# A macaron block with two routed expert layers: fewer steps of routing per group, deeper buffers for its scatters, and weight loads that wait for gathers

## The chip, the cores and the metric

The kernel runs on one core of one Trainium2 chip. The core has five engines that run their own instruction lists side by side and wait for each other through semaphores: TensorE (PE, matrix products and transposes), VectorE (DVE), ScalarE (ACT), GpSimd (POOL) and SyncE (SP), which here only issues transfers. Transfers (DMAs) run on 16 DMA engines that all queues share. The metric is the device time of the whole kernel in microseconds (us); lower is better. Everything is computed in float32, except for some small products of the softmax in bfloat16.

## The reference: what is computed

The input x has 8 sequences of 1024 rows of 512 numbers, so 8192 rows (tokens). Three residual steps follow each other:

```python
x = x + 0.5 * _L0_ffn_ref(_layernorm(x, axis=-1), w_router, w_gate, w_up, w_down)
x = x + _L0_attn_ref(_layernorm(x, axis=-1), Wq, bq, Wk, bk, Wv, bv, Wo, bo)
x = x + 0.5 * _L0_ffn_ref(_layernorm(x, axis=-1), w_router, w_gate, w_up, w_down)
```

The feed-forward step is a mixture of 32 experts, and each token goes to one of them, the one with the largest router logit. An expert takes at most C = 320 tokens, in the order of the tokens; a token beyond that gets only its own normalized row back. The expert's result is weighted by the token's softmax probability:

```python
logits = xt @ w_router
top1 = jnp.argmax(probs, axis=-1)
pos = jnp.cumsum(onehot, axis=0)[jnp.arange(T), top1] - 1
slot = jnp.where(pos < C, top1 * C + pos, E * C)
y = silu(buf @ w_gate) * (buf @ w_up) @ w_down        # per expert
```

The attention step is 16 heads of width 32 with rotary positions over each sequence.

## The kernel before, in words

The kernel has four stages in time: the front (0 to about 155 us of the profile) routes all tokens for the first expert layer; the first expert stage runs to about 960 us; attention to about 4065 us, and inside it the routing for the second layer; then the second expert stage until the end.

**The front** (`front`, L339) handles the 8192 tokens as 64 tiles of 128 rows. Its loop runs over the tiles with different parts of the work at different distances: SyncE loads four tiles at a time (`load(t)`, L353, 1 MB each, tile `xq`); VectorE takes mean and variance 12 tiles ahead (`stats`, L149: L151 and L152, tiles `st` and `mv`); for each group of 4 or 8 tiles `normalizing` (L154) makes the scale: VectorE adds the epsilon (`rstd`, L162), GpSimd raises to the power -0.5 (L163), VectorE makes `nmr` and two more (L165 to L167); ScalarE normalizes a tile to `h` (L172); TensorE transposes it (`tp`, L194); ScalarE, or for each eighth tile VectorE, copies the transposed tile to `xT` (L408); `routers` (L214) makes the logits of four tiles with two products (`pl` L223, `lp` L235) and copies (`parts` L230, `lg` L240).

Then `route` (L243) works on one group of 4 or 8 tiles. VectorE finds the maximum `mx`, the exponent's argument `ex`, the chosen expert as a one-hot row `oh`, and the running count `run` (L271 to L285). TensorE counts the tokens ahead of each one (`pp`, L290 and L294). VectorE makes from it the position `pos`, the table entry `row` (token number and gate, L304 and L305) and the place in the table, `slot` (L314 to L322), and for tokens beyond C the place `spare` (L324, L327). GpSimd scatters the entries into a table in HBM, one indirect transfer of 128 entries for each tile (L331). A group can start only when the group before has its `run`. There are ten groups, of 4, six times 8, and three times 4 tiles.

The routing is written as Python generators. Each `yield` ends a step, and `advance` (L391), which is called once in each turn of the loop over tiles, lets every open generator take one step. So a `yield` puts the rest of the routing into the next turn, behind the next tile's work, in each engine's list; engines work their lists strictly in order. The yields have three kinds (`WAIT`, `PE`, `DVE`), which the front does not tell apart. After the last tile `advance` is called until nothing is left.

After the last `run`, `sorted` (L433) sorts the experts by load (`keys` to `matrix`, then `order` and `arm`, L444 to L471). The order of the experts decides which weights are loaded first. An expert has three matrices, `wg`, `wu` and `wd`, of 1 MB each; `load` (L475) reads the expert's number into SyncE and issues three loads. After `front`, the weights of the first two experts of the first stage are loaded into a pool of their own (`et`, L1409 and L1430), so these loads stand in SyncE's list ahead of the stage. A load starts when SyncE reaches it and its buffer is free.

**An expert stage** (`experts`, L489) first reads the table back (`slots`, L553, issued by SyncE; it waits for the scatters), brings it into the experts' order with two small products (L557), and has the row numbers `come` and `go` (L559 to L564). Then for each expert GpSimd gathers its up to 320 rows with three indirect transfers (`gather`, L603, L609, tile `x`). `begin` (L568) normalizes and transposes the first expert's rows; it has three more powers on GpSimd. Then the loop over the experts: `feed` (L700) makes `gp` and `up` (L692) from the transposed rows `bT` and `wg`, `wu`, then `yp` (L731, L739) with `wd`, and prepares the next expert's rows meanwhile. In the loop the weights of expert r+1 are loaded and the rows of expert r+2 gathered. The pool `ew` (L509) has two sets of weights. In the first stage SyncE also loads each expert's share of all rows (`all`, L622) for the tokens beyond C, and GpSimd scatters them (L637); results are scattered at L749.

The orders of TensorE, ScalarE, VectorE and GpSimd are as written; SyncE's order is made by the framework's scheduler, which places an issue where its data and buffers are expected to be ready.

Of the kernel before, what the change touches and what calls it, by code (L numbers as in the profile page):

```python
# [13 lines left out]
F32 = mybir.dt.float32  # L14
I32 = mybir.dt.int32
# [7 lines left out]
P = 128  # L23
# [5 lines left out]
G = 8  # L29
# [3 lines left out]
WAIT, PE, DVE = "wait", "pe", "dve"  # L33
# [17 lines left out]
class Block:  # L51
# [191 lines left out]
    def route(  # L243
        self, t0, lg, pool, psum, tag, carry, table, spare=None, apart=False, counted=None
    ):

        nc, E, C, G = self.nc, self.E, self.C, lg.shape[1]
        rev = self.rev[:, 0:G, :]

        def wide(name):
            return pool.tile([P, G, E], F32, tag=name, bufs=2 if apart else 1, name=name)

        def narrow(name, dtype=F32):
            return pool.tile([P, G], dtype, tag=name, bufs=2, name=name)  # L260

        def over_e(x):
            return x.unsqueeze(2).to_broadcast([P, G, E])

        token = self.token[:, t0 : t0 + G]
        ex, oh = wide("ex"), wide("oh")
        mx, se, m = narrow("mx"), narrow("se"), narrow("m")

        row = pool.tile([P, G, 2], F32, tag="row", name="row")
        yield DVE, 1.5  # L270
        nc.vector.tensor_reduce(mx, lg, AX.X, ALU.max)  # L271

        nc.vector.tensor_tensor(ex, lg, over_e(mx), ALU.subtract)
        nc.scalar.activation(ex, ex, AF.Exp)
        nc.vector.tensor_tensor(lg, lg, over_e(mx), ALU.is_equal)
        nc.vector.tensor_tensor(lg, lg, rev, ALU.mult)
        yield DVE, 1.6
        nc.vector.tensor_reduce(m, lg, AX.X, ALU.max)
        nc.vector.tensor_tensor(oh, rev, over_e(m), ALU.is_equal)


        run = pool.tile([P, G + 1, E], F32, tag="run", bufs=2, name="run")
        nc.vector.tensor_copy(run[:, 0, :], carry)
        for j in range(G):
# [19 lines left out]
        nc.vector.tensor_scalar(row[:, :, 1], se, 0.5, None, ALU.mult)  # L304
        nc.vector.tensor_copy(row[:, :, 0], token)  # L305
        pos, s, u = narrow("pos"), narrow("s"), narrow("u")
        slot = narrow("slot", I32)
        nc.vector.tensor_reduce(pos, lg, AX.X, ALU.add)
        yield DVE, 1.5
        if order:  # L310
            at_once(order)

        tokens = slice(t0, t0 + G)
        nc.vector.tensor_scalar(u, pos, float(P), None, ALU.is_ge)  # L314
        for i in range(2, self.NB):
            nc.vector.scalar_tensor_tensor(u, pos, float(i * P), u, ALU.is_ge, ALU.add)
        nc.vector.scalar_tensor_tensor(s, m, float(-P), pos, ALU.mult, ALU.add)
        nc.vector.scalar_tensor_tensor(s, u, float((E - 1) * P), s, ALU.mult, ALU.add)

        nc.vector.tensor_tensor(s, s, self.away[:, tokens], ALU.subtract)  # L320
        nc.vector.scalar_tensor_tensor(s, pos, float(C), s, ALU.is_lt, ALU.mult)
        nc.vector.tensor_tensor(slot, s, self.past[:, tokens], ALU.add)  # L322
        if spare is not None:
            nc.vector.scalar_tensor_tensor(  # L324
                u, pos, float(C), self.beyond[:, tokens], ALU.is_ge, ALU.mult
            )
            nc.vector.tensor_scalar(spare[:, tokens], u, float(self.T), None, ALU.add)  # L327
        for j in range(G):
            if apart and j % 2 == 0:
                yield WAIT, 1  # L330
            nc.gpsimd.indirect_dma_start(  # L331
                out=table[t0 + j],
                out_offset=bass.IndirectOffsetOnAxis(ap=slot[:, j : j + 1], axis=0),
                in_=row[:, j, :],
                in_offset=None,
            )
        return run[:, G, :]

    def front(self, pool, psum, x, rest, spare, carry, table, ranked):  # L339
# [4 lines left out]
        nc, NT, D, KD, E = self.nc, self.NT, self.D, self.KD, self.E  # L344
# [4 lines left out]
        r, n = (pool.tile([P, NT], F32, name=name, bufs=1) for name in ("rstd", "nmr"))  # L349
# [2 lines left out]

        def load(t):  # L353
            xs[t // 4] = xq = pool.tile([P, 4, D], F32, tag="xq", bufs=7, name="xq")
            nc.sync.dma_start(
                xq, x[t * P : (t + 4) * P, :].rearrange("(j p) d -> p j d", p=P)
            )

        def tile_of(t):
            return xs[t // 4][:, t % 4, :]  # L360
# [7 lines left out]
        def routed(g):  # L368

            def counted(counts):  # L370
                state.carry = counts
                state.next += 1
                if state.next == len(sizes):
                    return ranked(counts)

            while state.next < g:
                yield
            yield from self.route(
                starts[g], lgs[g], pool, psum, "lp", state.carry, table, spare, True, counted
            )  # L380
# [10 lines left out]
        def advance():  # L391
            for steps in list(work):
                try:
                    next(steps)
                except StopIteration:
                    work.remove(steps)

# [4 lines left out]
        for i in range(-ahead, NT + 2):  # L402
# [3 lines left out]
            if late:  # L406
                to, from_, t = late
# [14 lines left out]
            t = i + ahead  # L422
# [49 lines left out]

        return (matrix, order, arm), rest()

    def load(self, pool, order, r, weights):  # L475

        nc = self.nc
        e = nc.values_load(
            order[0:1, r : r + 1], engines=[mybir.EngineType.SP], min_val=0,
            max_val=self.E - 1, skip_runtime_bounds_check_because="the number of a column of E",  # L480
        )
        tiles = []
        for name, w in zip(("wg", "wu", "wd"), weights):
            t = pool.tile([P, w.shape[1] // P, w.shape[2]], F32, tag=name, name=name)
            nc.sync.dma_start(t, w.rearrange("e (k p) f -> e p k f", p=P)[e])
            tiles.append(t)
        return tiles

    def experts(self, table, ranks, src, dst, weights, loaded=(), others=None):  # L489

# [7 lines left out]
        nc, tc, E = self.nc, self.tc, self.E  # L498
# [7 lines left out]
        for i in tc.Switch(which, len(self.profiles)):  # L506
            widths = self.profiles[i]
            with (
                tc.tile_pool(name="ew", bufs=2) as wp,  # L509
                tc.tile_pool(name="ea", bufs=2) as ap,  # L510
                tc.tile_pool(name="eps", bufs=2, space=PSUM) as ps,
                tc.manual_schedule(engines={F.PE, F.Activation, F.DVE, F.Pool}),
            ):
                expert = Expert(self, (wp, ap, ps), src, views, others)
                expert.places(table, matrix)

                def load(r):
                    return loaded[r] if r < len(loaded) else self.load(wp, order, r, weights)

                now = expert.gather(0, widths[0])  # L520
                now.weights = load(0)
                expert.begin(now)
                following = expert.gather(1, widths[1])
                for r in range(E):
                    if following:
                        following.weights = load(r + 1)
                    after = None
                    if r + 2 < E:
                        after = lambda: expert.gather(r + 2, widths[r + 2])
                    now, following = following, expert.feed(now, following, after)  # L530
# [842 lines left out]
def tile_macaron(  # L1373
# [3 lines left out]
    nc = tc.nc  # L1377
# [28 lines left out]

    F_ = mybir.EngineType
    first = ExitStack()
    et = first.enter_context(tc.tile_pool(name="et", bufs=2))  # L1409
    with (  # L1410
        tc.tile_pool(name="a", bufs=2) as pool,
        tc.tile_pool(name="aps", bufs=4, space=PSUM) as psum,
# [14 lines left out]
            return steps  # L1427

        s.front(pool, psum, xf, rest, spare, zero, dram_disjoint_views(tables[0], NT), ranked)
        loaded = [s.load(et, ranks[1], r, weights) for r in range(2)]  # L1430

    s.experts(tables[0], ranks, xf, x1, weights, loaded, (*rest, spare))
    first.close()
# [50 lines left out]
```

## Time and profile before

| what | us |
|---|---|
| time, median of 3 runs | 4916.72 (4915.27 to 4916.75) |
| profiled execution, its own time | 4919.01 |
| profiled execution, span | 4917.2 |
| TensorE busy in the span | 4646.1 (94%) |
| first statistics of a row (L151) | at 7.19 |
| first and last scatter of the first table (L331) | at 46.02 and 154.57 |
| first table read back (L553), issued | at 162.65 |
| first gather (L609), first product gp (L692) of the first stage | at 174.14 and 187.18 |
| last scatter of the second table | at 4074.51 |
| second table read back, issued | at 4077.49 |
| first gather, first product gp of the second stage | at 4082.05 and 4094.90 |
| granted clock of TensorE, mean | 0.971 |

The times in the lower rows count from the start of the span. A span is what the profiler saw between the first and the last instruction; the execution's own time is 1.8 us more. In the profile a line of the chain of work says what the last work was waiting for at that time; a "wait" names the instruction that came last of those waited for. The mark "issue" stands for time that no wait explains. The landing time of a transfer runs from its issue to the event that says that its data is there.

### The profile page before, as it was taken

What the parts mean: (1) busy time and instruction counts of PE and PEld (TensorE: products, weight loads), DVE (VectorE), ACT (ScalarE), POOL (GpSimd) and SP (SyncE); (2) the same over time, 40 slices, a digit from 0 to 9 for tenths busy, and PEclk for the clock granted to TensorE, in tenths of its full rate; (3) what the DMA queues carried; (4) which work ended last, traced back from release to release, by engine and by line L of the source; (5) the groups of instructions that cost most, each with busy time, mean ns of one, the idle gap of its engine ahead of it and who ended that gap; (6) DMA issues with size and microseconds to landing.
All of it is one profiled execution on the core that took longest, in us unless ns stands there. A gap on an engine that the chain in (4) does not pass through costs nothing.

```text
span 4917.2 us, 68877 instructions
## 1 busy us (share of the span) xinstructions
PE 4646.1 (94%) x24572; PEld 2133.2 (43%) x24572; DVE 2847.5 (58%) x5568; ACT 2925.1 (59%) x5856; POOL 789.9 (16%) x784
## 2 busy tenths in 40 slices
PE   7599999969899999999999999999999877999998
PEld 4366667723233333333333333333333224666676
DVE  8333333346666767777767767767777633333332
ACT  7121112118998888888888888888888831111111
POOL 4332333210000010110110010100001002222221
PEclk8799999979999999999999999999999988999999
DMA  4455556530111212212212212212212124445554
GB/s 140 154 171 169 195 181 212 193 91 22 37 31 55 76 38 67 70 42 64 69 42 66 70 40 67 70 38 67 63 46 57 48 67 164 161 155 170 169 183 135
DMA packets 290534, 486.03 MB, mean 99 GB/s; under 512 B 47847, under 2 KB 83121, under 8 KB 290176
## 3 DMA queue, kind: packets, MB, share of 16 engines
q1 hardware_dynamic: 255328, 404.36, 26.1%
q0 software_dynamic: 34560, 76.93, 5.1%
q8 instruction: 196, 3.21, 0.3%
q14 instruction: 162, 1.33, 0.1%
q10 hardware_dynamic: 288, 0.20, 0.0%
HBM read 380.11 MB, written 89.72 MB: 96 GB/s over the span
## 4 chain that ended last, share of the span: by engine, by line
PE 81%; DVE 8%; ACT 4%; issue 3%; DMA 2%; POOL 1%; SPq 1%; DVEq 0%; POOLq 0%; ACTq 0%
PE sa L1206 13%; PE gp L692 10%; PE up L692 9%; PE pq L1111 9%; PE po L1288 9%; PE yp L731 9%; PE sb L1186 5%; PE pv L1156 4%; PE px L1314 4%; PE sb L1213 3%; ACT junk L1225 2%; DVE nm L1221 2%; PE tp L680 2%; PE tp L194 1%; PE yp L739 1%
## 5 line engine op out<-in xcount | busy, mean ns | idle before, releaser
L1221 DVE TENSOR_REDUCE nm<-sa 128x2 f32<-128x1024 f32 x1024 | 1248.9, 1221 | 648.8 <-PE sa L1206 388.8
L1225 ACT ACTIVATE junk<-sa,nm 128x512 f32<-128x512 f32 x2048 | 1408.2, 688 | 256.2 <-DVE nm L1221 177.5
L1206 PE MATMUL sa<-k,q 32*128 32x512 f32 x4096 | 1150.0, 645 | 19.4 <-ACT junk L1225 12.0
L1218 ACT ACTIVATE pr<-sb 128x1024 f32<-128x1024 f32 x1024 | 1041.4, 1019 | 102.7 <-PE sb L1213 98.8
L1213 PE MATMUL sb<-q,k 32*128 32x512 f32 x4096 | 1063.2, 603 | 0.0
L697 ACT ACTIVATE sg<-gp 128x320 f32<-128x320 f32 (+3 forms) x256 | 102.9, 402 | 1231.2 <-PE gp L692 1081.3
L1136 POOL TENSOR_TENSOR raw<-raw,a 128x512 f32<-128x512 f32 x128 | 164.8, 1288 | 2398.7 <-DMA rot<-raw 1770.9
L1288 PE MATMUL po<-pr,v 128*32 128x512 f32 x4096 | 549.7, 608 | 0.1
L692 PE MATMUL gp<-bT,wg 128*128 128x320 f32 (+3 forms) x2048 | 533.4, 404 | 0.5 <-DVE bT L600 0.5
L692 PE MATMUL up<-bT,wu 128*128 128x320 f32 (+3 forms) x2048 | 525.8, 400 | 0.0
L1111 PE MATMUL pq<-hT,wqk 128*128 128x512 f32 x1024 | 511.4, 624 | 4.6 <-DVE raw L1126 3.6
L731 PE MATMUL yp<-wd,a 128*128 128x512 f32 x1024 | 453.7, 596 | 0.0
L692 PEld LDWEIGHTS gp<-bT,wg 128*128 128x128 f32 x2048 | 387.8, 191 | 116.7 <-issue 28.4
L1186 PE MATMUL sb<-mrow,ones 3*128 3x512 bf16 x2048 | 393.0, 385 | 40.4 <-ACT pr L1218 39.0
L692 PEld LDWEIGHTS up<-bT,wu 128*128 128x128 f32 x2048 | 389.8, 190 | 95.0 <-issue 1.4
L716 DVE TENSOR_TENSOR a<-sg,up 128x320 f32<-128x320 f32 (+3 forms) x256 | 114.1, 446 | 541.7 <-PE up L692 509.2
L1186 PEld LDWEIGHTS <-ones 3*128 3x128 bf16 x2048 | 99.6, 91 | 708.7 <-issue 668.4
L1225 ACT ACTIVATION_READ_ACCUMULATOR junk<-sa,nm 128x1 f32 x2048 | 398.1, 194 | 0.0
L1213 PEld LDWEIGHTS sb<-q,k 32*128 32x128 f32 x4096 | 359.9, 184 | 0.1
L1206 PEld LDWEIGHTS sa<-k,q 32*128 32x128 f32 x4096 | 305.1, 184 | 82.7 <-ACT pr L1218 31.3
L1111 PEld LDWEIGHTS pq<-hT,wqk 128*128 128x128 f32 x1024 | 176.2, 191 | 323.5 <-issue 227.4
L735 DVE SCALAR_TENSOR_TENSOR ys<-yp,gates,x 128x512 f32<-128x512 f32 x128 | 96.1, 751 | 369.0 <-PE yp L731 369.0
(176 smaller groups left out, 4277.4 us busy)
## 6 DMA issues: line engine op xcount, KB each, us to landing
wg<-in_w_gate SPq DMA_DIRECT2D x64, 1024.0 KB
wu<-in_w_up SPq DMA_DIRECT2D x64, 1024.0 KB
wd<-in_w_down SPq DMA_DIRECT2D x64, 1024.0 KB
rot<-raw SPq DMA_DIRECT2D x1024, 32.0 KB
xq<-in_x SPq DMA_DIRECT2D x16, 1024.0 KB
all<-in_x SPq DMA_DIRECT2D x32, 512.0 KB
xt<-first_rows SPq DMA_DIRECT2D x64, 256.0 KB
xr<-first_rows SPq DMA_DIRECT2D x64, 256.0 KB
```

The source lines that it names most:

```text
L692: nc.tensor.matmul(acc, w[:, k, f * P : (f + 1) * P], to.bT[:, k, 0:width], start=(k == 0), stop=(k == s.KD - 1),)
L731: nc.tensor.matmul(yp, a[:, f, i * P : (i + 1) * P], wd[:, f, :], start=(f == 0), stop=(f == KF - 1),)
L1111: nc.tensor.matmul(acc, w[:, which, k, :], self.hT[b, n][:, k, :], start=(k == 0), stop=(k == KD - 1),)
L1156: nc.tensor.matmul(acc, hT[:, k, at : at + P], self.w_vo[:, k, :], start=(k == 0), stop=(k == KD - 1),)
L1186: nc.tensor.matmul(sb[:, h, :], self.ones16[at : at + 3, :], row[at : at + 3, :], start=True, stop=False,)
L1206: nc.tensor.matmul(sa[:, h, :], qa[at, (g * 4 + j) * P : (g * 4 + j + 1) * P], ka[at, m * 512 : (m + 1) * 512], start=True, stop=True,)
L1213: nc.tensor.matmul(sb[:, h, :], k[at, t * P : (t + 1) * P], q[at, n * 512 : (n + 1) * 512], start=False, stop=True,)
L1218: nc.scalar.activation(pr, sb, AF.Exp)
L1221: nc.vector.tensor_reduce(nm[:, m, j, pair : pair + 2], sa, AX.X, ALU.max, negate=True)
L1225: nc.scalar.activation(self.junk, sa[:, h - pair, :], AF.Exp, bias=nm[:, m, j, h : h + 1], accum_out=se[:, m, j, h : h + 1],)
L1288: nc.tensor.matmul(self.po[at : at + HD, :], self.v[b][t][:, c * P + at : c * P + at + HD], prs[h // 2 * 2][:, h % 2, :], start=(t == 0), ...
L1314: nc.tensor.matmul(acc, self.oT[b, c, half][:, j * P : (j + 1) * P], self.w_vo[:, c, :], start=False, stop=(c == KD - 1),)
```

## The change

There are four edits in the front and two at the expert stages.

1. In the front, `advance` lets a generator run on over yields of the kinds `PE` and `DVE` and stops it only at a `WAIT`. One `WAIT` is added in `route`, between the two VectorE parts at the start. So routing of a group takes fewer turns of the loop. The waiting loop in `routed` yields a `WAIT` too.
2. In the front's routing, `row` and `slot` get four buffers each instead of two. In attention, where `route` is used as well, they keep two.
3. The first load of four tiles is split into four loads of one tile.
4. Only the first expert's weights are loaded after the front, not those of two; the pool `et` has one set.
5. In the first stage, the second expert's weights are loaded by the loop into `ew`. Its `wg` gets a GpSimd memset of one element first, which stands in GpSimd's list behind the second expert's gathers. The load writes the same tile, so it waits for the memset, and what stands behind it in SyncE's list waits too.
6. In the second stage, the first expert's `wu` gets such a memset behind the first expert's gathers, and the second expert's `wg` one behind the second expert's.

SyncE's list of the changed kernel has, at the first stage: the three loads of the first expert, the table's read, two loads of `all`, the three loads of the second expert, those of the third, and then one `all` and one expert in turn. Before, it had six loads, the table's read, one `all`, three loads, one `all`, three loads, two `all`. GpSimd's list before the first stage has 36 scatters ahead of the last group's power, where it had 28. The total number of GpSimd's scatters and of VectorE's instructions in the front is unchanged.

```diff
@@ route
+        deep = 4 if apart else 2
+
+        def narrow(name, dtype=F32, bufs=2):
+            return pool.tile([P, G], dtype, tag=name, bufs=bufs, name=name)
...
-        row = pool.tile([P, G, 2], F32, tag="row", name="row")
+        row = pool.tile([P, G, 2], F32, tag="row", bufs=deep, name="row")
...
         nc.vector.tensor_tensor(lg, lg, rev, ALU.mult)
+        if apart:
+            yield WAIT, 1
         yield DVE, 1.6
...
-        slot = narrow("slot", I32)
+        slot = narrow("slot", I32, deep)
@@ front
         def load(t):
             xs[t // 4] = xq = pool.tile([P, 4, D], F32, tag="xq", bufs=7, name="xq")
-            nc.sync.dma_start(
-                xq, x[t * P : (t + 4) * P, :].rearrange("(j p) d -> p j d", p=P)
-            )
+            n = 4 if t else 1
+            for j in range(0, 4, n):
+                nc.sync.dma_start(
+                    xq[:, j : j + n, :],
+                    x[(t + j) * P : (t + j + n) * P, :].rearrange("(j p) d -> p j d", p=P),
+                )
...
             while state.next < g:
-                yield
+                yield WAIT, 1
...
                 try:
-                    next(steps)
+
+                    while (next(steps) or (WAIT,))[0] != WAIT:
+                        pass
                 except StopIteration:
@@ load
-    def load(self, pool, order, r, weights):
+    def load(self, pool, order, r, weights, hold=None):
...
             t = pool.tile([P, w.shape[1] // P, w.shape[2]], F32, tag=name, name=name)
+            if name == hold:
+                nc.gpsimd.memset(t[0:1, 0, 0:1], 0.0)
             nc.sync.dma_start(t, w.rearrange("e (k p) f -> e p k f", p=P)[e])
@@ experts
-                def load(r):
-                    return loaded[r] if r < len(loaded) else self.load(wp, order, r, weights)
...
-                now.weights = load(0)
+                now.weights = loaded or self.load(wp, order, 0, weights, hold="wu")
                 expert.begin(now)
                 following = expert.gather(1, widths[1])
                 for r in range(E):
                     if following:
-                        following.weights = load(r + 1)
+                        following.weights = self.load(
+                            wp, order, r + 1, weights, hold=None if r else "wg"
+                        )
@@ tile_macaron
-    et = first.enter_context(tc.tile_pool(name="et", bufs=2))
+    et = first.enter_context(tc.tile_pool(name="et", bufs=1))
...
-        loaded = [s.load(et, ranks[1], r, weights) for r in range(2)]
+        loaded = s.load(et, ranks[1], 0, weights)
```

More of the change, by code (lines that the diff above doesn't have):

```diff
@@ L257, in wide @@
             return pool.tile([P, G, E], F32, tag=name, bufs=2 if apart else 1, name=name)
-        def narrow(name, dtype=F32):
-            return pool.tile([P, G], dtype, tag=name, bufs=2, name=name)
+        deep = 4 if apart else 2
+        def narrow(name, dtype=F32, bufs=2):
+            return pool.tile([P, G], dtype, tag=name, bufs=bufs, name=name)
         def over_e(x):
@@ L487, in load, with experts @@
         return tiles
-    def experts(self, table, ranks, src, dst, weights, loaded=(), others=None):
+    def experts(self, table, ranks, src, dst, weights, loaded=None, others=None):
         nc, tc, E = self.nc, self.tc, self.E
```

## The prediction

> **What bounds the kernel now.** I read the page first: TensorE has 81% of the chain of work that ended last, and the change touches none of its long stages.
>
> ```profile
> PE 81%; DVE 8%; ACT 4%; issue 3%; DMA 2%; POOL 1%; SPq 1%; DVEq 0%; POOLq 0%; ACTq 0%
> ```
>
> So what can be won lies where TensorE waits: before each of the two expert stages. I read the chain in order of time there (start, us, what). The first line group is before the first stage, the second before the other.
>
> ```profile
> 148.20 27.38 DMA table<-row,slot
> 175.58 6.17 DMA x<-in_x,come
> ...
> 187.18 4.63 PE gp L692 x8
> ...
> 4074.51 2.41 DMA table<-row,slot
> ...
> 4079.55 11.40 DMA wd<-in_w_down
> ...
> 4094.90 4.63 PE gp L692 x8
> ```
>
> From the last scatters of the routing table to the first product (gp) it takes 32.6 us the first time (last scatter issued at 154.57) and 20.4 us the second (4074.51), for the same work. The timeline shows what differs: SyncE's queue, with the six loads of two experts' weights in front of the read of the table.
>
> ```profile
> 150.07 3.53 SPq L485 DMA_DIRECT2D wu<-in_w_up  x1
> 153.79 3.51 SPq L485 DMA_DIRECT2D wd<-in_w_down  x1
> 162.65 0.35 SPq L553 DMA_DIRECT2D slots<-table  x1
> ...
> 171.54 0.22 DVE L554 COPY slots<-slots 32x128 f32<-32x128 f32 x1 [22.29 <-DMA slots<-table]
> ```
>
> The table's read takes 8.89 us to reach VectorE (162.65 to 171.54); the second time 2.04 us (4077.49 to 4079.53). Landing times of the table's scatters, from 100 to 140 us (no loads under way) and then from 146 to 162 us (loads):
>
> ```profile
> DMA to landing us min/median/max: 2.1/2.1/4.0
> ```
>
> ```profile
> DMA to landing us min/median/max: 2.1/7.0/8.4
> ```
>
> And of the gathers of rows: the first expert's three at 174 us, then those of a quiet stretch of the same stage (480 to 690 us):
>
> ```profile
> DMA to landing us min/median/max: 6.1/6.1/6.2
> ```
>
> ```profile
> DMA to landing us min/median/max: 3.3/3.5/5.4
> ```
>
> The second stage's first gathers land in 6.0 to 6.2 us too. For the routing itself I read VectorE's waits from 5 to 160 us (total, times, longest) and its busy time in a stretch of 16 us:
>
> ```profile
> DVE row L304 <- DMA table<-row,slot: 4.9, 2, 4.7
> DVE nmr L165 <- POOL rstd L163: 2.8, 6, 0.9
> ```
>
> ```profile
> 69.00:85.00 16.00, 13.70 (x73) 9.54 (x72) 14.62 (x54) 10.94 (x21) 10.08 (x10) 0.71 0.40 67
> ```
>
> The third busy time is VectorE's: 14.62 of 16. VectorE paces the front; ScalarE (10.94) and GpSimd (10.08) have room. At its end GpSimd does: a scatter each 1.275 us without a break.
>
> **What the Trainium skill says.** "DMA: Bandwidth & Descriptors", section "Queues, rings and completion order": each DMA engine takes turns between the queues that have work, a packet at a time. The trace agrees: a scatter of 1 KB lands in 2.1 us alone and in 7.0 us beside the weights. The same page, "Anatomy of one DMA — SWDGE (gpsimd) path", puts the fixed cost of a GpSimd DMA at about 2.0 us: the 2.1 agrees. "SBUF — State Buffer", "Who interferes with whom": some VectorE copies shut GpSimd out while they run. Scatters take 0.97 us, 1.16 at most, so moving them under other VectorE work is worth at most 0.2 us each; I take nothing.
>
> **Part 1: the first load in four pieces.** VectorE starts at 7.19, when 1 MB has landed. A quarter needs 0.79 MB less at about 380 GB/s: 2.1 us earlier. Three more issues by SyncE (0.4 us each) stand before the next load, whose data waits for the engines anyway; if not, they cost 1.2 us, on tiles that VectorE reaches 3 us later. VectorE's constants now stand behind the first rstd and cover its 0.45 us wait for GpSimd. Together -2.5 us.
>
> **Part 2: routing in fewer steps.** No instruction is removed: up to the sixth group's slots VectorE has 363 instructions in the changed order against 364, the difference being one copy of 0.6 us. What moves is GpSimd's order: a group's first two scatters now stand just ahead of the power (L163) for a later group. Slots at S let the scatters start at S+0.44; they end at S+2.7; rstd comes two tiles after S, at S+2.0, so the power starts at S+2.9, not S+2.25. VectorE's wait in nmr goes from 0.46 to 1.1 for four groups (+2.6); laid out in the same way, the next three wait 0.8, 0.5 and 1.6 where they waited for nothing (+2.9): +5.5. The sixth group's slots, at 116.4 before, come at 116.4 - 2.5 - 0.6 + 5.5 = 118.8. From there GpSimd has 28 scatters left and no gap: the last starts at 118.8 + 0.4 + 27 x 1.275 = 153.6, against 154.57: -1.0 us. Bounds: without the new waits the slots come at 113.3 and the last scatter at 148.1 (-6.4); with twice these waits, at 159.1 (+4.5).
>
> **Part 3: deeper row and slot buffers.** The 4.9 us wait of row goes. At the end one product (pp) has nothing between it and its reader: +0.9. Last slots: 148.8 - 2.5 + 5.5 - 4.9 + 0.9 = 147.8, and the order of the experts 2.2 earlier, at 145.6 (146.6 before). GpSimd reaches that group's four scatters only at 149.8, so this is worth nothing at the end: GpSimd's backlog hides it. Without that backlog the wait would be worth most of its 4.9.
>
> **Part 4: one expert loaded ahead, not two.** 3 MB from 146.0: 8.3 us of data at 380 GB/s after about 1.3 to start, so done by 155.6. SyncE's fifth and sixth issues, which took 3.5 us each instead of 0.38, are gone, and the table's read waits for the last scatter alone: 153.6 + 3.0 (as 4074.51 to 4077.49) + 0.6 for the end of the loads = 157.2, against 162.65. Then, each by the second hand-over's duration: 2.04 to land, 2.52 to the first gather, 2.57 to the third's issue, 3.5 for its landing in a quiet stretch, 4.06 from its statistics (183.12) to gp (187.18). gp starts at 171.9: **-15.3 us**. Two reads of the first rows (all, 0.5 MB each) stand behind the table's read and are through in 2.8 us, before the gathers start. The weights of the second expert wait for a GpSimd memset (some 0.1 us, by the MEMSET rows) behind the second expert's gathers, 3 us after gp; behind it on SyncE stand the next loads. 3 MB take 8.3 us and are wanted 31 us after gp (187.18 to 218.41): hidden. If the depth lost (two sets and one, where there were two and two) were not covered, TensorE would idle between experts; the second stage ran at that depth and gp idled 0.5 us over 2048 products.
>
> **Part 5: the hold in the second stage.** wu, wd and all of the second expert wait behind the first gathers. The landing falls from 6.2 to 3.5 us: **-2.7 us**, gp at 4092.2. wu is then issued at about 4086.5 and lands about 4 us later; up needs it at 4092.2 + 4.6. Slack 6 us. Bounds: 0 if wg alone disturbs as much, -3 at the 3.3 us minimum; a loss only if wu took over 10 us to land.
>
> **Sum**, against the profiled execution of 4919.0 us (span 4917.2): -18.0, so 4901.0; on the median of the runs, which is 2.3 us lower, 4898.7.
>
> **Rivals.** *The front gets shorter too* (0.22): GpSimd's powers slip between the scatters and the new waits stay away. For it: GpSimd idled 18.6 us in six gaps between 46 and 146 us. Against: two scatters are 2.55 us and the power comes 2.0 us after the slots. Last scatter at 148.1, so 5 us more: 4893.7. *The scatters still meet the weights* (0.15): the last ones run from 145 to 153 us, beside the 3 MB. If they land in 7 us as now, the read comes at 160.5 and some of the gathers' gain goes as well: some 6 us less, 4904.7. *Hidden anyway* (0.07): GpSimd's end slips by the 4 us above and the landings hold at 6; under 9 us are left, no change. *Slower* (0.06): VectorE stalls for the product pp. The change leaves two tiles' statistics (1.6 us) between the end of run and the reader of pp, and TensorE must do pp (1.2) and what stands ahead of it in that time. A stall of w in each of ten groups costs 10 w, less the 2.0 us by which GpSimd is behind at the end. It eats the gain at w = 2.0 and makes the kernel slower by 0.2% at 3.0: 4926.7. For that TensorE needs 4.6 us after run; pp with one transpose (0.65), one pl (1.06) and one lp (1.0) ahead makes 3.9. Against: in the trace pp waits for run (4.7 us over seven groups) and VectorE never for pp, so TensorE runs ahead.
>
> **How the numbers follow.** The main case has 0.50, with 4894 to 4903 as its own range. 0.2% is 9.8 us, about what a measurement here can tell. Faster: main, shorter front and nearly all of the third, 0.86; same 0.08; slower 0.06. The range 4890 to 4907 takes in the first rivals on both sides.
>
> **What would show it.** Right: first statistics at 5.1; nmr waiting longer, about 8 us in all; no wait of row; last scatter near 153; table read near 157 and its data 2 us later; gathers landing near 3.5 both times; first gp near 172, and the second one 2.7 us less after its last scatter. Wrong: gathers that still land in 6, a last scatter outside 148 to 158, lg waiting for pp, or gp or up waiting for weights.

## The result and the profile after

The changed kernel takes 4902.65 us (median of 10 runs, 4899.79 to 4905.07); the kernel before, run beside it, takes 4914.57 us (median of 10, 4911.83 to 4916.75). The ratio is 0.9976, with a 95% interval of 0.9966 to 0.9986: 11.9 us faster, where 18.0 was forecast. The direction and the range were right, and the size was half as large again as what came. Line numbers below are those of the kernel named; from `route` on, the changed kernel's are 3 to 13 higher than before's.

The profiled execution of the changed kernel has a span of 4899.7 us. Its chain of work, in order of time (start, us, what), ahead of the first stage and ahead of the second:

```profile
146.55 20.42 DMA table<-row,slot
...
167.73 3.54 DMA x<-in_x,come
...
175.35 4.63 PE gp L705 x8
```

```profile
4070.47 4.42 DMA x<-x,come
...
4078.98 3.69 PE gp L705 x8
```

The first product (gp) starts at 175.35 instead of 187.18. The gathers' link has shrunk from 6.17 to 3.54. The second stage's last gather lands in 4.42, which is neither the 6.2 of before nor the 3.5 of a quiet stretch. Just after it the memset opens the hold, and `wu` goes out:

```profile
4071.42 0.09 POOL L497 MEMSET wu<- 1x1 f32 x1
4071.53 0.39 SPq L498 DMA_DIRECT2D wu<-in_w_up  x1
```

The timeline of SyncE's queue and then VectorE's first use of the table:

```profile
148.39 0.39 SPq L498 DMA_DIRECT2D wg<-in_w_gate  x1
148.96 0.38 SPq L498 DMA_DIRECT2D wu<-in_w_up  x1
149.53 0.37 SPq L498 DMA_DIRECT2D wd<-in_w_down  x1
160.12 0.36 SPq L566 DMA_DIRECT2D slots<-table  x1
```

```profile
162.16 0.22 DVE L567 COPY slots<-slots 32x128 f32<-32x128 f32 x1 [12.06 <-DMA slots<-table]
```

The table's read now takes 2.04 us to reach VectorE (160.12 to 162.16), where it took 8.89. But it is issued 6.22 us after the last scatter (153.90), and 3.6 was forecast. What SyncE waited for there were the scatters (total, times, longest):

```profile
SPq L566 <- DMA table<-row,slot: 8.6, 3, 6.6
```

The landing times of the scatters tell why, first those from 100 to 140 us and then the six issued from 146 to 158 us:

```profile
DMA to landing us min/median/max: 2.1/2.1/3.0
```

```profile
DMA to landing us min/median/max: 2.1/4.3/6.6
```

The median of 4.3 mixes two kinds. The two scatters issued ahead of the first expert's loads (146.55 and 147.83) land in 2.1. Of the four issued beside these 3 MB (150.09 to 153.90) the profile has two landings, and both took 6.6.

In the front, VectorE's waits from 5 to 160 us (total, times, longest):

```profile
DVE nmr L165 <- POOL rstd L163: 5.9, 8, 1.2
DVE xT L418 <- PE tp L194: 2.2, 2, 1.4
DVE lg L305 <- PE pp L299: 1.2, 2, 0.7
...
DVE row L309 <- DMA table<-row,slot: 0.2, 1, 0.2
```

The wait for the scatters is gone (4.9 before), and as much is back as waits for GpSimd's power (2.8 to 5.9) and for TensorE (`xT` 1.3 to 2.2, `lg` none to 1.2). And GpSimd's timeline at the end of the front:

```profile
147.83 0.97 POOL L336 DMA_INDIRECT table<-row,slot  x1 [0.30 <-issue]
150.09 0.97 POOL L336 DMA_INDIRECT table<-row,slot  x1 [1.30 <-DVE spare L332]
...
153.90 0.97 POOL L336 DMA_INDIRECT table<-row,slot  x1 [0.30 <-issue]
```

GpSimd works off scatters, one each 1.27 us, until 147.83, then idles 1.30 us until the last group's places are there, and ends 0.67 us earlier than before. So the last group's scatters start when VectorE has their places, not when GpSimd's backlog is through.

The way from the last scatter to gp, piece by piece from the two timelines:

| piece | before | after | difference | forecast |
|---|---|---|---|---|
| last scatter issued at | 154.57 | 153.90 | -0.67 | -1.0 |
| from there to the table's read | 8.08 | 6.22 | -1.86 | -4.5 |
| read to its arrival at VectorE | 8.89 | 2.04 | -6.85 | -6.85 |
| arrival to the first gather | 2.60 | 2.70 | +0.10 | -0.1 |
| first gather to gp | 13.04 | 10.49 | -2.55 | -2.9 |
| first stage, sum | | | -11.83 | -15.3 |
| second stage, table's read to gp | 17.41 | 15.58 | -1.83 | -2.7 |

The two stages give -13.7 in the profiles. The medians differ by 11.9, the profiled spans by 17.5: the profiled execution of before, with its own time of 4919.01, is 4.4 us above the median of the runs beside the changed kernel. The 3.8 us between 17.5 and 13.7 lie in the long stages that the change does not touch, and I read nothing from them.

### The profile page after: what moved, and what is told of

It reads as the page before. It is cut to its first block, busy times and chain, and to the rows that moved or that the text cites. A ratio compares the mean times of both kernels' runs of the same rounds, so it can differ in the third digit from the quotient of the medians.

```text
span 4899.7 us, 68858 instructions
## 1 busy us (share of the span) xinstructions
PE 4644.6 (95%) x24572; PEld 2131.3 (43%) x24572; DVE 2848.9 (58%) x5568; ACT 2924.6 (60%) x5856; POOL 790.6 (16%) x787
## 4 chain that ended last, share of the span: by engine, by line
PE 82%; DVE 8%; ACT 4%; issue 3%; DMA 2%; POOL 1%; SPq 1%; DVEq 0%; POOLq 0%; ACTq 0%
PE sa L1219 13%; PE gp L705 10%; PE up L705 9%; PE pq L1124 9%; PE po L1301 9%; PE yp L744 9%; PE sb L1199 6%; PE px L1327 4%; PE pv L1169 4%; PE sb L1226 3%; ACT junk L1238 2%; DVE nm L1234 2%; PE tp L693 2%; PE tp L194 1%; PE yp L752 1%
## 5 line engine op out<-in xcount | busy, mean ns | idle before, releaser
L705 PEld LDWEIGHTS gp<-bT,wg 128*128 128x128 f32 x2048 | 387.5, 191 | 116.4 <-issue 28.1
```

The lines of the kernel that those rows point to most:

```text
L705: nc.tensor.matmul(acc, w[:, k, f * P : (f + 1) * P], to.bT[:, k, 0:width], start=(k == 0), stop=(k == s.KD - 1),)
```

## The experiments

Three sets of four kernels were run. The kernels of one set shared a chip and the runs of the kernel before, which took 4913.6 us in the first set, 4930.1 in the second and 4928.5 in the third. Each kernel is therefore held against the kernel before of its own set, and positions in the profile are compared inside a set. The first two sets did not have the changed kernel; there its times and positions are those of the result above, where the kernel before took 4914.6 us, and such a comparison is across sets.

Two theories stood at the start. Mine: nearly all of the gain is in the loads, and what is missing of it is the last scatters' landing beside the first expert's weights. The rival: the front's edits carry a good part of the gain, and the loads less than I said.

### Set 1: which part gives the gain

**The front's edits alone** (edits 1 to 3; loads of two experts ahead and no memsets, as before):

```diff
-    et = first.enter_context(tc.tile_pool(name="et", bufs=1))
+    et = first.enter_context(tc.tile_pool(name="et", bufs=2))
-        loaded = s.load(et, ranks[1], 0, weights)
+        loaded = [s.load(et, ranks[1], r, weights) for r in range(2)]
-                now.weights = loaded or self.load(wp, order, 0, weights, hold="wu")
+                now.weights = load(0)
```

> Edits 1 to 3 alone (fewer steps, deeper buffers, split first load); the weights of two experts are loaded ahead and nothing is held, as before. My theory (the front's end is set by GpSimd's scatters, and the gain comes from the loads): last scatter at 153 to 154.5, table read issued at 161 to 163, first gp at 185 to 187, second hand-over as before (17.4 us from the table's read to gp); time 0 to 2 us under the kernel before. Rival (the shorter routing is what pays): last scatter before 150 and at least 6 us gained.

4916.27 us (13 runs), ratio 1.0003 (0.9995 to 1.0011): no gain. SyncE's queue shows the old pattern back, a sixth load that takes 6.49 us to issue, with the read behind it:

```profile
152.56 6.49 SPq L498 DMA_DIRECT2D wd<-in_w_down  x1
160.74 2.58 SPq L567 DMA_DIRECT2D slots<-table  x1
```

The last scatter is at 154.48, as before and as expected. The read took 12.15 us to reach VectorE (8.89 before), so gp came at 188.51, 1.3 us later than before, where 185 to 187 had been expected.

**The loads' edits alone** (edits 4 to 6 with the front of before; shown against the changed kernel, in part):

```diff
-            n = 4 if t else 1
-            for j in range(0, 4, n):
-                nc.sync.dma_start(...)
+            nc.sync.dma_start(xq, ...)
-                    while (next(steps) or (WAIT,))[0] != WAIT:
-                        pass
+                    next(steps)
-        deep = 4 if apart else 2
```

> Edits 4 to 6 alone (one expert ahead, the rest held); the front as before. My theory: last scatter at 154.6 as before, table read at 160 to 161, first gp at 175 to 177, table's read to gp in the second stage 15.6 us; 11 to 13 us gained, nearly all of the change. Rival: less than 6 us gained, because the scatters end no sooner and the table's read waits for them in any case.

4900.75 us (8 runs), ratio 0.9975 (0.9964 to 0.9986), -12.8 us: the whole gain. Last scatter at 154.15, the table's read at 159.70, gp at 174.76; in the second stage 15.37 from read to gp (4061.01 to 4076.38). So the three edits of the front together give nothing that these medians resolve, alone or on top (their intervals are 8 to 11 us wide).

**The first expert's weights held as well** (changed kernel, diff in part; in the first stage, too, nothing is loaded before the first gathers have been given out):

```diff
-        loaded = s.load(et, ranks[1], 0, weights)
-    s.experts(tables[0], ranks, xf, x1, weights, loaded, (*rest, spare))
+    s.experts(tables[0], ranks, xf, x1, weights, None, (*rest, spare))
-                now.weights = loaded or self.load(wp, order, 0, weights, hold="wu")
+                now.weights = loaded or self.load(wp, order, 0, weights, hold="wg" if others else "wu")
```

> The changed kernel with the first expert's weights of the first stage held too, behind that expert's gathers. My theory (the table's read is late because the last scatters share the engines with the first expert's 3 MB): scatters land in 2.1 to 2.5 us, table read 3.0 us after the last scatter, at 157, first gp at 171.5 to 172.5, 3 us better than the changed kernel. Rival (the read waits for something else, such as SyncE's branch): read still at 159 or later and gp at 174 or later; or gp waits for wg and comes later than 175.4.

4897.39 us (6 runs), ratio 0.9968 (0.9955 to 0.998), -16.2 us. SyncE's queue, and the chain of work:

```profile
156.05 0.35 SPq L566 DMA_DIRECT2D slots<-table  x1
...
164.61 0.39 SPq L498 DMA_DIRECT2D wg<-in_w_gate  x1
```

```profile
146.08 16.70 DMA table<-row,slot
...
163.54 3.54 DMA x<-in_x,come
...
171.21 4.61 PE gp L705 x8
```

The last scatter is at 153.43, and the read follows 2.62 us later instead of 6.22. The scatters from 146 us on land like those of the quiet stretch:

```profile
DMA to landing us min/median/max: 2.1/2.2/3.2
```

gp starts 4.14 us earlier than in the changed kernel, of which 0.47 is the scatter's. The first expert's weights, issued 16 us later, make no wait: from the first gather to gp it takes 10.53 us, where it took 10.49. This confirms the missing term and its size. The two times, 16.2 and 11.9 us below the kernel before, have overlapping intervals. In the second stage, where nothing was changed, this profile has 16.58 from read to gp (15.58 in the changed kernel's), with the last gather landing in 5.38.

**The power ahead of a group's scatters** (changed kernel, with one more turn of the loop before the first scatter):

```diff
+        if apart:
+            yield WAIT, 1
         for j in range(G):
             if apart and j % 2 == 0:
                 yield WAIT, 1
```

> The changed kernel with one more turn before a group's first scatter, so that GpSimd's power for the later group stands ahead of the scatters. My theory (VectorE waits in nmr because two scatters stand ahead of the power): nmr waits 3 us or less in all instead of 6.3, the sixth group's slots at 114 to 115.5 instead of 117.7, last scatter at 150 to 151.5 instead of 153.9, first gp 2 to 3.5 us earlier. Rival (the power is late for another reason): nmr waits stay over 5 us and the last scatter at 153 to 154.5.

4906.54 us (21 runs), ratio 0.9985 (0.9978 to 0.9991): faster than before by 7, and by the medians behind the changed kernel's 11.9, with overlapping intervals. A gain over the changed kernel had been expected: a wait for the power of 3 us or less, a last scatter at 150 to 151.5 and an earlier gp. For the groups of 8 the wait for the power fell to 0.3 or 0.4 from 0.7 to 1.0. For two others the extra turn put the power behind eight scatters, and they waited 3.0 and 3.9:

```profile
DVE nmr L165 <- POOL rstd L163: 9.3, 7, 3.9
```

So the cause is right (a power waits for the scatters ahead of it), and the kernel was a bad test of its price: it moved the wait. Last scatter at 155.89, gp at 179.52. Only 2.0 of the 4.2 us that gp lost against the changed kernel are the scatter's: another 2.0 were lost because here the table's read came 8.24 us after it, not 6.22, with these last scatters landing in up to 8.0 us beside the loads.

### Set 2: the pieces

In this set every kernel's front ends some 10 us later, from waits of VectorE for TensorE towards the end of the front, which the last section tells of.

**One scatter in a turn** instead of two (changed kernel):

```diff
-            if apart and j % 2 == 0:
+            if apart:
                 yield WAIT, 1
```

> The changed kernel with one scatter to a turn instead of two, so that one scatter at most stands ahead of any power. My theory (VectorE's waits in nmr come from the scatters that stand ahead of the power, two in the changed kernel, eight for the short groups where all are put behind one another): nmr waits 2.3 to 3.2 us in all instead of 6, the sixth group's slots at 113.8 to 115.5, last scatter at 150 to 152.5, first gp 1.5 to 3.5 us before the changed kernel's 175.35. Rival (the waits have another cause, or the time lost there is regained elsewhere): slots of the sixth group at 117 or later, last scatter at 153 to 156.

```profile
DVE nmr L165 <- POOL rstd L163: 2.5, 5, 0.9
```

The wait for the power is 2.5 us in all, down from about 6, and the sixth group's places come at 115.04 (117.72 in the changed kernel's profile of the first result). That was expected, and it puts a price on the two scatters. Time 4909.87 (5 runs), ratio 0.996 (0.9947 to 0.9974), -20.3 us. The last scatter at 161.71 and gp at 183.28 miss what had been expected (150 to 152.5, and earlier than 175.35), because of the waits of this set.

**The front of before with all weights held** (edits 4 to 6, and the first expert's weights too; against the kernel before, in part):

```diff
-        loaded = [s.load(et, ranks[1], r, weights) for r in range(2)]
+                now.weights = loaded or self.load(wp, order, 0, weights, hold="wg" if others else "wu")
```

> The front as before; no weights ahead of the first stage, those of the first expert wait behind its gathers, the second's behind its own. My theory (all of the gain lies in keeping weights away from scatters, table read and gathers; the edits of the front give about 1 us): last scatter at 154 to 154.6, table read at 157 to 157.6, first gp at 172 to 173, time 15 to 17 us under the kernel before and within 2 us of the same loads with the new front. Rival (the new front is needed for it): 5 us or more behind the same loads with the new front.

4911.52 us (5 runs), ratio 0.9964 (0.995 to 0.9977), -18.6 us. The read stands 2.62 us behind the last scatter again (169.01 and 171.63), the second time that holding gives this number. The read had been expected at 157 to 157.6, and missed that with the whole front. Its front ends 4 to 7 us later than the other fronts of this set, so with this wait present the front's edits seem to be worth something in the profile; the medians, with intervals of up to 13 us, don't resolve it. Whether it comes within 2 us of the same loads behind the new front stays open, since no such kernel is in this set.

**No memsets** (changed kernel; one expert loaded ahead, nothing held):

```diff
-weights, hold="wu")
+weights, hold=None)
-wp, order, r + 1, weights, hold=None if r else "wg"
+wp, order, r + 1, weights, hold=None
```

> The changed kernel without the two memsets: one expert is loaded ahead, but the second expert's weights of the first stage and the first two of the second stage wait for nothing. My theory (a gather beside weights lands in 6 us, not 3.5): table read at 160 as in the changed kernel, gathers landing in 5.5 to 6.2 us both times, from the table's read to gp 17 to 18 us in both stages (15.2 and 15.6 with the holds); 3.5 to 5 us slower than the changed kernel. Rival (weights queued behind the table's read do not reach the gathers): under 1 us slower.

4917.60 us (11 runs), ratio 0.9976 (0.9967 to 0.9985), -12.5 us. SyncE's queue and the chain:

```profile
171.04 0.36 SPq L566 DMA_DIRECT2D slots<-table  x1
171.93 0.39 SPq L498 DMA_DIRECT2D wg<-in_w_gate  x1
```

```profile
178.61 6.84 DMA x<-in_x,come
...
189.55 3.99 PE gp L705 x8
```

Without the hold the second expert's weights go out 0.9 us after the table's read, and the third gather lands in 6.84 instead of 3.54. From read to gp it takes 18.51 us in the first stage (15.23 with the hold) and 17.66 in the second (15.58): by these profiles the holds are worth 3.3 and 2.1 us, where 3.5 to 5 had been expected for both together. What is left of the gain fits the table's read, which now stands in SyncE's queue behind three loads instead of six.

**Two buffers for row and slot** (changed kernel, one run):

```diff
-        deep = 4 if apart else 2
+        deep = 2
```

> The changed kernel with two row and slot buffers instead of four. My theory (with fewer steps the scatters of the group before last are through when row is written, so the deeper buffers save nothing): row waits for scatters 0.3 to 0.8 us in all, last scatter at 153.9 to 154.6. Rival (the buffers are what removed the 4.9 us wait): row waits 4 us or more.

4911.11 us in one run. The deep buffers can't be told from the shallow ones here: no wait of row for a scatter came back, VectorE's waits being

```profile
DVE lg L305 <- remote: 6.6, 1, 6.6
DVE lg L305 <- PE tp L194: 5.0, 1, 5.0
DVE nmr L165 <- POOL rstd L163: 4.3, 6, 1.0
```

In this set VectorE stands still 11.6 us for TensorE in just that stretch, and the scatters may use this time to land. The last scatter, expected at 153.9 to 154.6, is at 164.98. What the deep buffers are worth without this wait stays open. Set 1 does not settle it: with the loads' edits alone, so without deep buffers, the time was no longer than the changed kernel's, but there the other edits of the front were gone as well.

### Set 3: the changed kernel, the missing term again, and two edits together

**The changed kernel itself:**

> The changed kernel itself, as the measure for the three others of this set. Expected: 11 to 13 us below the kernel before; first statistics at 4.2 to 4.3; first stage's table read 6.2 us after the last scatter's issue, from the read to the first product 15.2; second stage 15.6. If the stages are set by the chip and not by the code, the TensorE wait of some 12 us near 140 us that all four kernels of the second set had (and none of the first) either appears in all four kernels of this set or in none.

4912.35 us (7 runs, 4911.33 to 4916.29), ratio 0.9968 (0.9957 to 0.9979), -16.1 us. Last scatter at 163.89, read 6.27 us later, gp at 185.16, 15.00 us after the read; in the second stage 15.55. The stages repeat to 0.3 us; the gain of 16.1 against the 11 to 13 expected misses, and the two intervals overlap.

**The first expert's weights held**, the kernel of set 1 again:

> The changed kernel with the first expert's weights, too, held until its gathers have been given out, beside the changed kernel on one chip. Theory (the last scatters' landing beside these 3 MB is what the forecast of -18 missed): read 2.6 us after the last scatter's issue instead of 6.2, first product 3.5 to 4.5 earlier than the changed kernel's, time 3 to 5 us below it. Rival (its earlier lead came from runs at a luckier time): within 1 us of the changed kernel.

4909.24 us (5 runs), ratio 0.9961 (0.9948 to 0.9975), 3.1 us below the changed kernel. Read 2.62 us after the last scatter, gp 4.41 us earlier, of which 0.83 is the scatter's. Both as expected. The intervals of the two times overlap; what shows the effect is the profile, the second time now.

**Held, and one scatter in a turn** (the two diffs together):

> The kernel with the held first weights, with one scatter in a turn in place of two, so that a group's power stands behind one scatter. If the first stage's end is set by GpSimd's backlog of scatters from the sixth group on (as in the first set): slots of the sixth group at 115 instead of 117.7, the last scatter 2.5 to 2.9 us earlier, the first product as much earlier, time 2 to 3 us below the kernel with held weights. If VectorE's wait for TensorE near 140 us sets it (as in the second set): the last scatter within 0.5 us or later, since fewer scatters have been given out by then, and no gain or a loss of up to 3 us.

4906.65 us (5 runs, 4902.82 to 4907.69), ratio 0.9955 (0.9941 to 0.9968), -21.8 us. No run of it is as slow as the fastest of the changed kernel. Waits of VectorE and SyncE's queue:

```profile
DVE lg L305 <- remote: 9.0, 2, 4.8
...
DVE nmr L165 <- POOL rstd L163: 2.5, 5, 0.9
```

```profile
162.71 0.35 SPq L566 DMA_DIRECT2D slots<-table  x1
163.11 0.94 SPq L635 DMA_DIRECT2D all<-in_x  x2
171.30 0.39 SPq L498 DMA_DIRECT2D wg<-in_w_gate  x1
```

The sixth group's places come at 114.46 (118.21 with two scatters in a turn), the last scatter at 160.09 (163.06) and gp at 177.74 (180.75), so 3.0 us earlier; the time is 2.6 us below that of the kernel with held weights. This is what was expected of a front that GpSimd's backlog ends. But here VectorE's wait for TensorE ends it, and for that case no gain was expected: VectorE itself arrives at the two parts of this wait 3.4 and 3.7 us earlier, so that the wait did not eat the gain. My either-or was too narrow. Against the kernel before of its set this version is the fastest of the twelve. One more set would be needed to give the difference to the changed kernel (5.7 us) an interval of its own.

**The first load in one piece** (changed kernel):

```diff
-            n = 4 if t else 1
+            n = 4
```

> The changed kernel with the first block of x loaded in one piece again. My first part (four pieces are worth 2.5 us at the first scatter, and all of it arrives at the end of the front): first statistics at 7.1 to 7.2 instead of 4.24, first scatter at 40.3 to 40.7 instead of 38.1, last scatter and first product 2 to 2.7 later than the changed kernel's. Rival (the wait moves to later tiles of the first block, or to the constants): first scatter within 0.8 us of 38.1 and the end within 0.5.

First statistics at 6.99 (4.22 in four pieces), first scatter at 39.88 (37.99), last scatter at 166.21 (163.89), gp at 187.49 (185.16). The four pieces win 2.8 us at the start, 1.9 at the first scatter, and 2.3 at gp. The first statistics are 0.1 and the first scatter 0.4 earlier than I had expected; what is won at the first scatter arrives at the end. The medians, 4912.56 (6 runs) and 4912.35, are too coarse to show it.

## Why the prediction was right, and where its sizes were off

**Part 4, the loads: right in its mechanism, one term too small.** Three of its links came out as laid out: the read's landing (2.04 forecast, 2.04 measured), the way to the first gather (2.52, 2.70) and from gather to gp (10.13, 10.49). The step that failed is "the table's read waits for the last scatter alone: 153.6 + 3.0 + 0.6 for the end of the loads". The 0.6 measured 3.2: 6.22 less 3.0. My own layout had the first expert's loads run from 146.0 to 155.6 and the scatters until 153.6, so side by side, and still I gave the last one the landing time of a scatter that meets almost nothing. The loads were in fact issued at 148.39 to 149.53, over 2 us later than laid out, and they met all four scatters of that group (150.09 to 153.90). Holding these loads brought the 6.2 us down to 2.62, by 3.60 against the changed kernel's first profile and by 3.65 inside the third set. With 3.2 instead of 0.6 Part 4 would have been -12.7; measured is -11.8. That is the rival *The scatters still meet the weights*, which said 160.5 for the read (160.12 measured) and 4904.7 for the kernel. Its mechanism is what the trace shows; only its second half, that the gathers' gain goes as well, is wrong (3.54 us). So it is in part luck that its total, a gain of 12.0 us, is so close to the 11.9 measured. The mechanism is also what the Trainium skill's page "DMA: Bandwidth & Descriptors", section "Queues, rings and completion order", leads one to expect (engines take turns between queues that have work): here a scatter of 1 KB takes 2.1 us alone and 6.6 beside 3 MB. I used it for the scatters of before, and for those of after only in this rival, to which I gave 0.15.

**Part 5: right in its direction, and too large by a third of what was forecast.** -2.7 forecast, -1.83 measured, and 2.1 by taking the memsets away. The landing of 3.5 us was the wrong figure. A memset behind the gathers in GpSimd's list holds the loads until the gathers have been *issued*, not landed: the last gather is issued at 4070.47 and `wu` at 4071.53, so it lands beside `wu` and `wd`, in 4.42 us. The difference of 6.2 and 4.4 is the 1.8 measured. In the first stage the hold sits behind the second expert's gathers, so the first expert's are through: there the 3.5 holds. But the order of issues alone does not give the 0.9 us that are missing. In the four kernels that hold the first expert's weights in the first stage, `wg` goes out just as soon, 1.1 us after the third gather (163.54 and 164.61 above), and that gather lands in 3.37 to 3.54. In the second stage the last gather took 4.19 to 5.38 in the eleven profiles with the hold, and read to gp 15.37 to 16.58, against 17.41 to 17.98 in the three without it. So the hold's worth there lies between 0.8 and 2.6 us by single profiles, and why the second stage's gather suffers and the first stage's does not stays open.

**Part 1: right.** 2.5 forecast and 2.3 measured at the first product. First statistics came at 4.24, earlier than the 5.1 I had laid out. The next tiles' pieces then took two waits of 0.5 us, so that it is nearly the same further on.

**Part 2: right in its mechanism, too dear.** The wait for the power rose from 2.8 to 5.9 us; 2.8 + 5.5 = 8.3 had been forecast. The groups waited 0.2 to 1.2 us where I had 0.5 to 1.6. The sixth group's places came at 117.72 (118.8 forecast, 116.4 before) and the last scatter at 153.90 (153.6). One scatter in a turn instead of two takes the wait down to 2.5, and with held weights 3.0 us off the first product: this shows that GpSimd's scatters ahead of the powers are what it costs.

**Part 3: its small worth is not refuted, nor shown by itself.** The wait of row went (4.9 to 0.2), waits for TensorE came (lg 1.2, forecast 0.9; xT 0.9 more), and nothing was left at the end. The reason I gave, a backlog of GpSimd without a gap that hides VectorE's end, fails at the very end: after gaps of 0.59 and 1.30 the last four scatters waited for VectorE, as the last places came at 149.65 rather than at 147.8. That the last scatter still came at 153.90, where 153.6 was forecast, is in part luck: the sixth group's places came 1.1 us sooner than laid out and the last group's 1.9 us later. So a longer wait on VectorE would have shown in the last scatter here. The runs with and without deep buffers don't separate them.

**The sum.** Part 4 was too large by 3.5 and Part 5 by 0.9: 4.4 of the 6.1 us by which the forecast missed. The other 1.7 is within what the medians are certain to (their interval is 6.9 to 16.7 us; the forecast of 18.0 lies outside it). The front's edits alone showed no gain (ratio 1.0003): Part 1's 2.3 us were lost again, by the profile mostly to Part 2's waits. The slower rival, VectorE stalling for the product pp, did not come in this form: 0.7 us was the longest such wait.

## What to carry to other kernels

Find who else is on the DMA engines in the last microseconds before a hand-over, where one stage waits for another's results: here each hand-over lost some two to four microseconds when its small scatters and gathers met megabytes that nobody needed yet. A one-element memset behind the gathers on the issuing engine is a cheap hold for those loads (0.09 us), but it opens when the gathers are issued, so the last one can still meet the loads. When deferring work by turns in an in-order list, count what is put ahead of the small operation that another engine waits for; two scatters of 1.27 us ahead of each power, in place of one, cost 3 us over this front, by one pair of profiles.

## What the runs showed that was not expected

In all eight kernels of the second and third set the last scatter comes at 160.1 to 169.0 us; in those of the first set and in the profiles of before and after it came at 153.4 to 155.9. Here are VectorE's waits from 100 to 165 us for the changed kernel in set 3, to be held against the waits in the section on the result (`lg` waited 1.2 there):

```profile
DVE lg L305 <- remote: 8.3, 2, 4.8
DVE nmr L165 <- POOL rstd L163: 1.4, 2, 1.2
```

The mark "remote" names no instruction of this core. VectorE waits for the product `pp`, which the trace of TensorE has as done 3 to 6 us earlier (in the kernel with two buffers it ends at 143.68 and is read at 149.64). With the front of before the same kind of wait shows as 12.7 us of `xT` for `tp`. The kernel is the same in the two profiles of the changed kernel. With the wait the last scatter is at 163.89 instead of 153.90 and gp at 185.16 instead of 175.35. That is 9.8 us, and the medians of the two differ by 9.7. The added waits of `lg` are 7.1 us of it, and the 9.8 us at gp are nearly all by which the changed kernel was slower in that set. For the kernel before, which was 13.9 us slower there, no profile of that set was taken. So the larger gains of the second and third set (12.5 to 21.8 us) may hold a part that belongs to this wait. The wait is in all kernels of a set or in none, though the first and the third set were run on the same chip by number. What holds TensorE back was not found, and no run was made for it. For a change whose worth lies in the front it matters: where the wait is present, VectorE's end and not GpSimd's backlog sets the last scatter.
